# A graph neural network in fp32 on one core: two pairs of node chunks of the graph product in seven block products, results' additions and the norm's statistics re-ordered

## The chip, the core and the metric

The kernel runs on one core of one Trainium2 chip. Its engines are TensorE (PE in the profile, with its weight loads as PEld), VectorE (DVE), ScalarE (ACT), GpSimd (POOL) and SyncE (SP), which issues most of the DMAs. The metric is the device time of one execution in microseconds (us); lower is better.

## The reference, cut to what matters

Two layers work on x of 16 batches x 1024 nodes x 256 channels. The change touches layer 0: its graph product g, its queries q and keys k, and the norm that begins layer 1.

```python
h = jnp.maximum(_layernorm(x, axis=-1), 0.0)
x = x + _L0_gnn_ref(h, para, adj, kv_w)        # layer 0, below
h = jnp.maximum(_layernorm(x, axis=-1), 0.0)   # layer 1's norm
x = x + _L1_gnn_ref(h, adj, W1, ...)           # A_hat product, linear, batchnorm, relu, linear, batchnorm

# layer 0, for B=16, N=1024, C=256, 4 heads of 64
fea = jnp.transpose(h, (0, 2, 1))
c_adj = jnp.mean(fea, axis=1)
diff = c_adj[:, None, :] - c_adj[:, :, None]
A = jnp.abs(jnp.abs(jax.nn.sigmoid(diff) - 0.5) - 0.5) * 2.0
Wg = adj[None, :, :] * (A + jnp.transpose(A, (0, 2, 1))) * 0.5
g = jax.nn.relu(jnp.einsum('bcn,bnm->bcm', fea, Wg) * para.reshape(1, C, N))
q = heads(transpose(g));  k, v = heads(h @ kv_w)
attn = jax.nn.softmax(jnp.einsum('bhnd,bhmd->bhnm', q, k) * scale, axis=-1)
out = jnp.einsum('bhnm,bhmd->bhnd', attn, v)   # added to x
```

## The kernel before

All data are fp32. Each batch is worked on with its 1024 nodes in eight chunks of 128 partitions and its 256 channels in two halves. The loop over batches b has three large stages on TensorE: the attention of batch b, then `graph(b + 1)`, which makes the next batch's queries, values and keys, then linear 1 of batch b (`linear1` and `linear1_seven`), which is layer 1's A_hat product and its first linear layer.

Every engine works in the order in which the Python code issues to it: the batch loop stands in a manual schedule over all five engines, so an instruction waits for the one in front of it on its engine, and each DMA issued by SP for the one issued before it. Tiles come from pools; a tag with n buffers is used in turn, and a new tile waits until the last reader of the old one in its buffer is done.

The graph product takes, for each chunk c, a weight tile w of 128 x 1024. ScalarE makes it with Abs and Tanh, VectorE multiplies it with the chunk of adj (`weights`, L342 to L351). The tag "w4" holds five such tiles. `graph` (L375) loops over the eight chunks; before each chunk's products it runs steps handed over in the dictionary `between` (L1140 to L1152), among them the making of later w tiles, the end of the attention before it (`left`: add of the first results, collect, invert, spread, scale, add of the second results) and the norm of batch b (`norm.stats`, `norm.invert`, `norm.relu`). Each chunk has four matmuls of 128 x 128 by 128 x 512 into two PSUM tiles gps, accumulated over the eight chunks (L399).

`turn_h` transposes h: VectorE in blocks of 32, then 32 DMAs of 32 KB from the GpSimd queue into the two tiles hT, which keys and values read. The results of the attention are turned in a like way by 16 DMAs from SP (`scale`, L596 to L616) into a tile att, and added to x (L618).

After the eight chunks `queries` multiplies gps with para (two tiles from "w4", loaded by SP at chunk 5) and applies a ReLU (L416, L417). `values` makes v in two halves of 16 matmuls of 256 columns, each copied by ScalarE. From batch 2 on the keys come from seven block products instead of eight (L455 to L493), with differences of hT made by VectorE (L460 to L465) and sums of the weights loaded from DRAM: four of the products are accumulated on one running sum x in PSUM, which ScalarE copies each time a block of the result is complete in it.

[...]the tag "s" has three tiles of two banks (gps, halves of values, key products, attention scores, linear 1), "o" and "t" one bank each.

In linear 1 the A_hat product is also one of seven block products (L694 to L763). Between its products stand steps for batch b + 2: the statistics of its first norm (`prepare_start`), on x loaded by `arrive`, and the ReLU of that norm (`prepare_end`, eight ScalarE activations, L279). `arrive` reuses the tile that `leave` has stored to DRAM. ScalarE's copies L745, L749, L756 and L762 take the running sum away between the products.

Of the kernel before, what the change touches and what calls it, by code (L numbers as in the profile page):

```python
# [10 lines left out]
F32 = mybir.dt.float32  # L11
AF = mybir.ActivationFunctionType
# [5 lines left out]
P = 128  # L18
# [11 lines left out]
def fast_path(  # L30
# [143 lines left out]
    with ExitStack() as stage:  # L174
# [167 lines left out]
        def weights(b, c):  # L342


            w = w4.tile([P, N], F32, tag="w4", name=f"f_w_{b}_{c}")
            nc.scalar.activation(  # L346
                w, rows[b], AF.Abs, bias=cols[b][:, c : c + 1], scale=0.5 / C
            )
            nc.scalar.activation(w, w, AF.Tanh)  # L349
            nc.vector.scalar_tensor_tensor(w, w, 1.0, adj_t[c], ALU.subtract, ALU.mult)  # L350
            ws[b, c] = w  # L351

        hTs = {}

# [20 lines left out]
        def graph(b, between):  # L375


            gps = [ps_s.tile([P, N], F32, tag="s", name=f"f_gps_{b}_{d}") for d in range(CC)]
            hT = None
            para_t = []  # L380
            for c in range(NC):
                for step in between.get(c, ()):
                    step()
                if c == 5:
                    for d in range(CC):
                        t = w4.tile([P, N], F32, tag="w4", name=f"f_para_{b}_{d}")
                        nc.sync.dma_start(t, para_v[:, d, :])
                        para_t.append(t)
                if c == 6 and b > 1:
                    t23 = pp.tile([P, 2, 512], F32, tag="acc", name=f"f_kt23_{b}", bufs=2)  # L390
                    rest = pp.tile([P, 2, 512], F32, tag="acc", name=f"f_kt4_{b}", bufs=2)
                    sums = rest[:, 1].rearrange("p (n q) -> p n q", n=4)
                    nc.sync.dma_start(sums, kvs_d)
                w = ws.pop((b, c))
                blocks = [(d, g) for d in range(CC) for g in range(NH)]
                if b == 0 and c == 0:
                    blocks.sort(key=lambda n: n[1])
                for d, g in blocks:
                    nc.tensor.matmul(  # L399
                        gps[d][:, ts(g, 512)],  # L400
                        hs[b][:, c, ts(d, P)],
                        w[:, ts(g, 512)],
                        start=(c == 0),
                        stop=(c == NC - 1),
                    )
                if c == 0:
                    hT = hTs.pop(b)
            for step in between.get(NC, ()):
                step()
            kT = big.tile([P, CC, N], F32, tag="kT", name=f"f_kT_{b}")  # L410
            qT = big.tile([P, CC, N], F32, tag="qT", name=f"f_qT_{b}")
            v = big.tile([P, NC, C], F32, tag="v", name=f"f_v_{b}")

            def queries(d):

                nc.vector.tensor_mul(qT[:, d, :], gps[d], para_t[d])  # L416
                nc.scalar.activation(qT[:, d, :], qT[:, d, :], AF.Relu, scale=-SCALE)  # L417

            def values():
                for c4 in range(0, NC, 4):  # L420
                    ps = ps_s.tile([P, 4, C], F32, tag="s", name=f"f_vps_{b}_{c4}")
                    for i in range(4):
                        for e in range(CC):
                            nc.tensor.matmul(  # L424
                                ps[:, i, :],
                                hT[e][:, ts(c4 + i, P)],
                                kvw_t[:, e, C : 2 * C],
                                start=(e == 0),
                                stop=(e == CC - 1),
                            )  # L430
                    nc.scalar.copy(v[:, c4 : c4 + 4, :], ps)

            late = between.get("late", ())
            if b < 2:
                for step in late:
                    step()
                for d in range(CC):
                    ps = ps_s.tile([P, N], F32, tag="s", name=f"f_kps_{b}_{d}")
                    for g in range(NH):
                        for e in range(CC):  # L440
                            nc.tensor.matmul(  # L441
                                ps[:, ts(g, 512)],
                                kvw_t[:, e, ts(d, P)],
                                hT[e][:, ts(g, 512)],
                                start=(e == 0),
                                stop=(e == CC - 1),
                            )
                    nc.scalar.copy(kT[:, d, :], ps)
                    queries(d)
                values()  # L450
                return qT, kT, v

            t2, t3, t4 = t23[:, 0], t23[:, 1], rest[:, 0]  # L455
            part = lambda k, j: hT[k][:, ts(j, 512)]
            a = lambda i, k: kvw_t[:, k, ts(i, P)]
            for d in range(CC):
                queries(d)
            nc.vector.tensor_sub(t3, part(1, 1), part(0, 1))  # L460
            nc.vector.tensor_add(t2, t3, part(0, 0))
            nc.vector.tensor_sub(t4, part(1, 0), t2)
            values()
            t1 = part(0, 1)
            nc.vector.tensor_sub(t1, t1, part(0, 0))  # L465

            def mult(ps, left, right, more=False):
                nc.tensor.matmul(  # L468
                    ps, left, right, start=not more, stop=True, skip_group_check=more
                )  # L470

            c = lambda i, j: kT[:, i, ts(j, 512)]
            x = ps_s.tile([P, 512], F32, tag="s", name=f"f_kpsx_{b}")
            m7 = ps_s.tile([P, 512], F32, tag="s", name=f"f_kps7_{b}")
            m2 = ps_t.tile([P, 512], F32, tag="t", name=f"f_kps2_{b}")
            m4 = ps_o.tile([P, 512], F32, tag="o", name=f"f_kps4_{b}")
            mult(x, a(0, 0), part(0, 0))
            nc.scalar.copy(c(0, 0), x)
            mult(m2, a(0, 1), part(1, 0))
            nc.vector.tensor_add(c(0, 0), c(0, 0), m2)  # L480
            late[0]()
            mult(x, sums[:, 1], t2, True)
            nc.scalar.copy(c(1, 0), x)
            late[1]()
            mult(m7, sums[:, 2], t3)
            nc.vector.tensor_add(c(1, 0), c(1, 0), m7)
            mult(x, sums[:, 0], t1, True)
            nc.scalar.copy(c(1, 1), x)
            mult(m4, a(1, 1), t4)
            nc.vector.tensor_add(c(1, 1), c(1, 1), m7)  # L490
            nc.vector.tensor_add(c(1, 0), c(1, 0), m4)
            mult(x, sums[:, 3], part(1, 1), True)
            nc.scalar.copy(c(0, 1), x)  # L493
            return qT, kT, v

        def attention(b, qT, kT, v, hooks):

# [68 lines left out]
            def finish(g):  # L566
# [29 lines left out]
                def scale():  # L596
                    oT = oT_of.pop(g)
                    blocks = oT.rearrange("p h j c i -> p (h j c) i")
                    nc.vector.tensor_mul(
                        blocks,  # L600
                        blocks,
                        kept["recs"]
                        .rearrange("p h j c -> p (h j c)")
                        .unsqueeze(2)
                        .to_broadcast([P, 16 * HEADS // 2, 32]),
                    )
                    t = ow.tile(
                        [P, HEADS // 2, 4, 4, 32], F32, tag="att", name=f"f_att_{b}_{g}"
                    )
                    for a in range(4):  # L610
                        for j in range(4):
                            nc.sync.dma_start(
                                t[ts(j, 32), :, a].rearrange("r h c i -> r h (c i)"),
                                oT[ts(a, 32), :, j].rearrange("r h c i -> r h (c i)"),
                            )
                    kept["att"] = t  # L616
# [430 lines left out]
        with tc.manual_schedule(engines={ENG.PE, ENG.Activation, ENG.DVE, ENG.Pool, ENG.SP}):  # L1047
# [73 lines left out]
            for b in range(B):  # L1121
# [35 lines left out]
                if b + 1 < B:  # L1157
                    if 0 < b < B - 2:
                        thirds = load_thirds(b)
                    qkv = graph(b + 1, between)  # L1160
                    if b == 0:
                        for step in scale[4:]:
                            step()
                        thirds = make_thirds(b)
                if b + 2 < B:
# [1 line left out]
                        b,  # L1167
                        norm.h,
                        thirds,
                        lambda: prepare_start(b + 2),  # L1170
                        lambda: prepare_end(b + 2),
                        lambda: (prepare_row(b + 2), again(b + 1)),
                    )
# [932 lines left out]
```

## Time and profile before

| what | value |
|---|---|
| time, median of 3 runs | 2425.27 us (2425.07 to 2425.58) |
| the profiled execution | 2425.91 us |
| its span, first to last instruction | 2424.1 us |
| granted TensorE clock, mean | 0.995 |
| PE / DVE / ACT / POOL busy in the span | 2384.8 / 1781.2 / 1325.8 / 308.6 us |
| graph matmuls (L399), records | 1024, busy 444.7 us |
| one batch of the loop, graph(3) to graph(4) | 389.1 to 522.4 us of the span |
| of it VectorE busy in the attention, 466.0 to 522.4 | 53.3 us |

The page lists busy time per engine, then the chain of work that ended last, followed back from the last instruction. One program matmul in fp32 appears as two records. A line number such as L399 is that of the kernel printed above. Times inside the trace count from the span's start; a window row gives start:end, its length, and then for each engine the busy time with the number of instructions in brackets, the TensorE clock, the share of the DMA engines and GB/s.

### The profile page before, as it was taken

To read this page: it belongs to the slowest core of one execution; us is meant where nothing else is said; L and a number is where in the kernel's file an instruction comes from. 1 tells how busy PE (TensorE), PEld (TensorE's weight loads), DVE (VectorE), ACT (ScalarE), POOL (GpSimd) and SP (SyncE) were. 2 spreads that over 40 slices of the span, in tenths; PEclk is the share of its full clock that TensorE was granted. 3 is DMA by queue.
4 is the path that set the end of the run, shared out by engine and by line. 5 is a ranking of instruction groups with operands and counts; after the bars stand their busy time and mean duration, and the time that the engine had idled before them with its cause. 6 is when DMAs were issued, how large, how long until landed. Compare 5 with 4: busy or idle time off the path is not lost.

```text
span 2424.1 us, 24651 instructions
## 1 busy us (share of the span) xinstructions
PE 2384.8 (98%) x8034; PEld 1050.7 (43%) x8034; DVE 1781.2 (73%) x2442; ACT 1325.8 (55%) x1932; POOL 308.6 (13%) x547
## 2 busy tenths in 40 slices
PE   8999999999999999999999999999999999999995
PEld 4453444434343434444343434344443434444444
DVE  6878778685959586786859595877868596757766
ACT  6845555464646455554646464555546465446654
POOL 2030202021020302020200203020202011000000
PEclk9999999999999999999999999999999999999998
DMA  5041414222332414142323324142423222355569
GB/s 187 9 140 61 152 61 126 87 88 74 115 95 62 146 61 152 61 126 87 89 73 115 95 63 146 61 152 61 126 87 88 73 68 85 101 192 195 176 239 375
DMA packets 176633, 275.76 MB, mean 114 GB/s; under 512 B 37872, under 2 KB 121328, under 8 KB 176496
## 3 DMA queue, kind: packets, MB, share of 16 engines
q1 hardware_dynamic: 156336, 241.55, 30.7%
q0 software_dynamic: 15552, 15.77, 2.5%
q10 hardware_dynamic: 4608, 16.78, 1.7%
q8 instruction: 66, 1.08, 0.2%
q14 instruction: 71, 0.58, 0.1%
HBM read 169.35 MB, written 71.10 MB: 99 GB/s over the span
## 4 chain that ended last, share of the span: by engine, by line
PE 93%; DVE 3%; DMA 2%; issue 1%; SPq 1%; POOL 0%; ACT 0%; DVEq 0%; ACTq 0%; POOLq 0%
PE f_s L507 17%; PE f_o L548 17%; PE f_gps L399 17%; PE f_aps L704 16%; PE f_zps L810 6%; PE f_vps L424 4%; PE f_zx L1326 4%; PE f_zm L1326 3%; PE f_kpsx L468 2%; PE f_kps L468 1%; DVE f_acc L524 1%; PE f_outps L1546 1%; PE f_z2ps L1264 1%; PE f_kps L441 1%; PE f_zps L892 1%
## 5 line engine op out<-in xcount | busy, mean ns | idle before, releaser
L515 ACT ACTIVATE f_p<-f_s 128x1024 f32<-128x1024 f32 x512 | 477.3, 1046 | 151.8 <-PE f_s L507 151.7
L524 DVE TENSOR_TENSOR f_acc<-f_acc,f_p 128x1024 f32<-128x1024 f32 x384 | 470.5, 1225 | 41.1 <-ACT f_p L515 0.5
L507 PE MATMUL f_s<-f_qT,f_kT 64*128 64x512 f32 x2048 | 456.8, 596 | 0.0
L548 PE MATMUL f_o<-f_p,f_v 128*64 128x512 f32 x2048 | 453.6, 595 | 0.0
L399 PE MATMUL f_gps<-f_w,f_h_a 128*128 128x512 f32 x1024 | 444.7, 594 | 0.3 <-DVE f_w L337 0.3
L369 POOL DMA_DIRECT2D f_hT<-f_hQ x480 | 235.9, 499 | 1221.7 <-PE f_gps L399 1170.8
L507 PEld LDWEIGHTS f_s<-f_qT,f_kT 64*128 64x128 f32 x2048 | 190.7, 185 | 263.6 <-ACT f_p L515 117.1
L399 PEld LDWEIGHTS f_gps<-f_w,f_h_a 128*128 128x128 f32 x1024 | 192.8, 190 | 247.0 <-issue 230.0
L548 PEld LDWEIGHTS f_o<-f_p,f_v 128*64 128x64 f32 x2048 | 141.4, 137 | 304.3 <-issue 254.2
L350 DVE SCALAR_TENSOR_TENSOR f_w<-f_w,f_adj 128x1024 f32<-128x1024 f32 x127 | 153.8, 1212 | 39.1 <-ACT f_w L349 39.1
L346 ACT ACTIVATE f_w<-f_row,f_col 128x1024 f32<-128x1024 f32 x127 | 147.0, 1157 | 29.3 <-DMA f_row<-frow 28.5
L279 ACT ACTIVATE f_h_b<-f_x,f_shift_b,f_rstd_b 128x256 f32<-128x256 f32 x128 | 67.9, 594 | 162.5 <-DVE f_shift_b L264 162.5
L349 ACT ACTIVATE f_w<-f_w 128x1024 f32<-128x1024 f32 x127 | 134.3, 1057 | 4.0
L704 PE MATMUL f_aps<-f_ahatT,f_hs 128*128 128x512 f32 x256 | 115.1, 592 | 0.0
L424 PE MATMUL f_vps<-f_kvw,f_hT 128*128 128x256 f32 x512 | 113.4, 379 | 0.2 <-DVE f_qT L416 0.2
L704 PE MATMUL f_aps<-f_ahatT,f_h_b 128*128 128x512 f32 x256 | 112.7, 593 | 0.0
L704 PE MATMUL f_aps<-f_t,f_hs 128*128 128x512 f32 x256 | 112.5, 592 | 0.0
L279 ACT ACTIVATE f_h_a<-f_x,f_shift_a,f_rstd_a 128x256 f32<-128x256 f32 x126 | 73.8, 587 | 62.6 <-DVE f_shift_a L264 62.6
L424 PEld LDWEIGHTS f_vps<-f_kvw,f_hT 128*128 128x128 f32 x512 | 97.2, 190 | 20.6 <-issue 7.4
L521 DVE TENSOR_TENSOR f_acc<-f_p,f_p 128x1024 f32<-128x1024 f32 x64 | 76.2, 1191 | 15.3 <-ACT f_p L515 15.3
L590 ACT COPY f_recs<-f_rec 32x32 f32<-32x32 f32 x128 | 31.5, 246 | 98.7 <-DVE f_rec L582 97.5
L575 ACT COPY f_parts<-f_red 32x64 f32<-32x64 f32 x128 | 39.0, 305 | 78.5 <-DVE f_red L540 77.3
(230 smaller groups left out, 2705.7 us busy)
## 6 DMA issues: line engine op xcount, KB each, us to landing
f_t<-ft SPq DMA_DIRECT2D x84, 512.0 KB, 6.9
fz<-f_z SPq DMA_DIRECT2D x64, 512.0 KB, 9.9
f_x<-in_x_dram SPq DMA_DIRECT2D x31, 1024.0 KB, 5.9
f_zb<-fz SPq DMA_DIRECT2D x42, 512.0 KB, 4.2
f_para<-in_L_gnn_para_dram SPq DMA_DIRECT2D x32, 512.0 KB, 4.5
f_att<-f_oT SPq DMA_DIRECT2D x512, 32.0 KB, 1.9
fx<-f_x SPq DMA_DIRECT2D x16, 1024.0 KB, 6.5
f_hT<-f_hQ POOLq DMA_DIRECT2D x480, 32.0 KB, 2.6
```

The costliest lines, as they stand in the source:

```text
L346: nc.scalar.activation(w, rows[b], AF.Abs, bias=cols[b][:, c : c + 1], scale=0.5 / C)
L350: nc.vector.scalar_tensor_tensor(w, w, 1.0, adj_t[c], ALU.subtract, ALU.mult)
L369: queue.dma_start(to[ts(k, 32), ts(a, 32 * NC)], t[ts(a, 32), k].rearrange("i c r -> i (c r)"),)
L399: nc.tensor.matmul(gps[d][:, ts(g, 512)], hs[b][:, c, ts(d, P)], w[:, ts(g, 512)], start=(c == 0), stop=(c == NC - 1),)
L424: nc.tensor.matmul(ps[:, i, :], hT[e][:, ts(c4 + i, P)], kvw_t[:, e, C : 2 * C], start=(e == 0), stop=(e == CC - 1),)
L507: nc.tensor.matmul(ps[:, e, :], kT[rows_e, pair, ts(m, P)], qT[rows_e, pair, ts(g, 512)], start=True, stop=True,)
L515: nc.scalar.activation(p, ps, AF.Exp)
L524: nc.vector.tensor_add(acc_of[s], acc_of[s], p)
L548: nc.tensor.matmul(o_of[s][e * HD : (e + 1) * HD, :], v[:, m, ts(2 * pair + e, HD)], p[:, e, :], start=(m == 0), stop=(m == NC - 1),)
L704: nc.tensor.matmul(ps, left[:, m, :], right(m), start=not more and m == 0, stop=(m == KH - 1), skip_group_check=more,)
L810: nc.tensor.matmul(ps[i], left[:, ts(i, P)], right, start=not more, stop=True, skip_group_check=more,)
L1326: nc.tensor.matmul(ps, left[:, m, :], right[:, m, :], start=start and m == 0, stop=(m == 1), skip_group_check=not start,)
```

## The change

For batches 2 to 15 `graph` is replaced by `graph_seven`; batches 0 and 1 keep `graph`. The statements' order in it is the order on each engine.

- Chunks 0 to 3 are accumulated as before. Chunks 4 to 7 form two pairs n = 0, 1. For each pair the 2 x 2 block product (channel halves by node halves, summed over the two chunks) is made from seven products with sums s of h and differences t of w, and the products of the two pairs are accumulated.
- s1 to s4 (256 columns each) are made by VectorE in the tag "sums". Of the t's, t2 and t3 lie in the still unused kT, t1 and t4 overwrite parts of w.
- A running sum in the "t" bank is copied by ScalarE three times into the still unused v (`room`), and m7 stands in the "o" bank. VectorE then adds m7 twice, adds gps, and multiplies by para, which is loaded in one DMA into qT itself, ahead of the results' DMAs.
- The ReLU of the queries is done later: one half among the key products, the other in linear 1 (`todo`), for the last batch both among the key products.
- The first results' addition comes after the t's, the second in front of the multiplication of the second half by para, behind the keys' differences. The second results' tile takes the tag "oT" in place of "att".
- The norm's statistics, root, shifts and ReLU go by halves: chunks 0 to 3 after the graph product, chunks 4 to 7 among the key products, its ReLU at their end. `leave` and `arrive` are issued among the key products.

```diff
+        def graph_seven(b, left, norm, last):
+            gps = [ps_s.tile([P, N], F32, tag="s", name=f"f_gps_{b}_{d}") for d in range(CC)]
+            add0, collect, invert, spread, scale, add1 = left
+            h = hs[b]
...
+            turn_h(b)
+            differences(b, 2)
+            masked(b, 2)
+            collect()
+            invert()
+            differences(b, 3)
+            masked(b, 3)
+            differences(b, 4)
+            qT = big.tile([P, CC, N], F32, tag="qT", name=f"f_qT_{b}")
+            nc.sync.dma_start(qT, para_v)
+            spread()
+            scale()
+            masked(b, 4)
+            plain(0)
+            differences(b, 5)
+            masked(b, 5)
...
+            room = v.rearrange("p (n k) c -> p n (k c)", n=4)
+            nc.vector.tensor_sub(s3, a(0, 0), a(1, 0))
+            nc.vector.tensor_add(s1, a(1, 0), a(1, 1))
+            nc.vector.tensor_sub(s2, s1, a(0, 0))
+            nc.vector.tensor_sub(s4, a(0, 1), s2)
+            plain(1)
+            differences(b, 6)
+            masked(b, 6)
+            make_t3(0)
+            make_t1(0)
+            plain(2)
+            differences(b, 7)
+            masked(b, 7)
+            make_t2(0)
+            plain(3)
...
+            make_t3(1)
+            make_t1(1)
+            make_t2(1)
...
+            m1(0)
+            m2(0)
+            m1(1)
+            nc.scalar.copy(room[:, 0], x)
+            m_7(0)
+            m3(0)
+            m2(1)
+            make_t4(0)
+            make_t4(1)
+            m6(0)
+            m_7(1)
+            m3(1)
+            m6(1)
+            nc.scalar.copy(room[:, 2], x)
+            m4(0)
+            m4(1)
+            m5(0)
+            m5(1)
+            nc.scalar.copy(room[:, 1], x)
+            add0()
+            nc.vector.tensor_add(room[:, 2], room[:, 2], m7)
+            norm.stats(0, 4)
+            norm.invert(0, 4)
+            nc.vector.tensor_add(room[:, 3], room[:, 1], m7)
+            for d in range(CC):
+                nc.vector.tensor_add(both(d), both(d), gps[d])
...
+            nc.vector.tensor_mul(qT[:, 0, :], both(0), qT[:, 0, :])
+            norm.shifts(0, 4)
+            norm.relu(0, 4, False)
+            copy0, copy1 = values(b, hT, v)
+            copy0()
+            nc.vector.tensor_sub(kt3, part(1, 1), part(0, 1))
+            nc.vector.tensor_add(kt2, kt3, part(0, 0))
+            nc.vector.tensor_sub(kt4, part(1, 0), kt2)
+            nc.vector.tensor_sub(kt1, kt1, part(0, 0))
+            add1()
+            nc.vector.tensor_mul(qT[:, 1, :], both(1), qT[:, 1, :])
+            norm.stats(4, NC)
+            norm.invert(4, NC)
...
             nc.vector.tensor_add(c(0, 0), c(0, 0), k2)
-            late[0]()
+            leave(b - 1)
+            arrive(b + 1)
             mult(x, sums[:, 1], kt2, True)
             nc.scalar.copy(c(1, 0), x)
-            late[1]()
+            todo.pop(0)()
             mult(m7, sums[:, 2], kt3)
             nc.vector.tensor_add(c(1, 0), c(1, 0), m7)
             mult(x, sums[:, 0], kt1, True)
             nc.scalar.copy(c(1, 1), x)
+            copy1()
             mult(k4, aw(1, 1), kt4)
             nc.vector.tensor_add(c(1, 1), c(1, 1), m7)
+            norm.shifts(4, NC)
             nc.vector.tensor_add(c(1, 0), c(1, 0), k4)
             mult(x, sums[:, 3], part(1, 1), True)
             nc.scalar.copy(c(0, 1), x)
-            return qT, kT, v
+            if last:
+                todo.pop(0)()
+            norm.relu(4, NC, False)
+            return (qT, kT, v), todo
...
-                        [P, HEADS // 2, 4, 4, 32], F32, tag="att", name=f"f_att_{b}_{g}"
+                        tag="att" if g == 0 else "oT",
...
-                    qkv = graph(b + 1, between)
+                    if b == 0:
+                        qkv = graph(b + 1, between)
+                        todo = []
+                    else:
+                        qkv, todo = graph_seven(b + 1, left, norm, b + 2 == B)
...
-                        lambda: prepare_start(b + 2),
+                        lambda: ([step() for step in todo], prepare_start(b + 2)),
```

The products and differences that `graph_seven` calls, for pair n, where a(i, k) is channel half i of h in the pair's chunk k, and part_w(n, k, j) node half j of that chunk's w:

```python
make_t3: t3[n] = part_w(n, 1, 1) - part_w(n, 0, 1)
make_t1: t1[n] = part_w(n, 0, 1) - part_w(n, 0, 0)   # in place
make_t2: t2[n] = part_w(n, 1, 1) - t1[n]
make_t4: t4[n] = part_w(n, 1, 0) - t2[n]             # in place
m1: x += a(0,0) part_w(n,0,0)      m2: gps[0] half 0 += a(0,1) part_w(n,1,0)
m_7: m7 += s3 t3[n]                m3: gps[0] half 1 += s4 part_w(n,1,1)
m6: x += s2 t2[n]                  m4: gps[1] half 0 += a(1,1) t4[n]
m5: x += s1 t1[n]
```

## The prediction

> **What bounds the kernel now.** I read the page's busy shares first, then the chain of waits that ended last, then the waits of TensorE, and then one batch by stages and engine by engine.
>
> ```profile
> PE 2384.8 (98%) x8034; PEld 1050.7 (43%) x8034; DVE 1781.2 (73%) x2442; ACT 1325.8 (55%) x1932; POOL 308.6 (13%) x547
> PE 93%; DVE 3%; DMA 2%; issue 1%; SPq 1%; POOL 0%; ACT 0%; DVEq 0%; ACTq 0%; POOLq 0%
> PE f_s L507 17%; PE f_o L548 17%; PE f_gps L399 17%; PE f_aps L704 16%; PE f_zps L810 6%; PE f_vps L424 4%; PE f_zx L1326 4%; PE f_zm L1326 3%; PE f_kpsx L468 2%; PE f_kps L468 1%; DVE f_acc L524 1%; PE f_outps L1546 1%; PE f_z2ps L1264 1%; PE f_kps L441 1%; PE f_zps L892 1%
> ```
>
> [...] Here the chain says it too: 93% of it is PE. From graph(2) on the chain repeats every 133.3 us, one batch; this is graph(3) with what follows (start, length, what):
>
> ```profile
> 389.15 27.66 PE f_gps L399 x64
> 416.82 6.91 PE f_vps L424 x32
> ...
> 430.04 24.03 PE f_aps L704 x56
> 454.08 10.30 PE f_zps L810 x24
> ```
>
> The reader is to see that these pieces abut. The windows of that batch (graph product, values, keys, two linear-1 parts, attention; columns PE, PEld, DVE, ACT, POOL busy) have PE busy in every microsecond:
>
> ```profile
> 389.10:416.70 27.60, 27.60 (x67) 12.29 (x66) 20.25 (x37) 13.49 (x20) 17.38 (x33) 1.00 0.76 235
> 416.70:423.60 6.90, 6.90 (x34) 6.07 (x33) 3.88 (x6) 4.38 (x6) 0.00 (x0) 1.00 0.28 99
> 423.60:429.90 6.30, 6.30 (x16) 2.40 (x15) 2.81 (x5) 4.65 (x8) 0.00 (x0) 1.00 0.11 16
> 429.90:453.90 24.00, 24.00 (x57) 10.62 (x56) 8.94 (x27) 7.00 (x20) 1.64 (x1) 1.00 0.17 61
> ```
>
> So matmuls taken out shorten the run one for one, as long as VectorE (DVE) keeps up: it is busy 20.25+3.88+2.81 = 26.9 of the 40.8 us from graph product to last key product.
>
> **Prices.** [...] 32 graph matmuls in the program are 64 records in 27.66 us, 0.864 us each. [...] an fp32 add: 0.69 us at 512 (trace 0.69), 1.22 at 1024 (trace 1.22)[...]. Independent neighbours start closer together in the trace (0.60 and 1.13 us).
>
> **The change, part by part,** for each of the 14 batches 2 to 15 (graph(0) and graph(1) keep the old form).
>
> 1. TensorE. Four chunks stay at 4 matmuls each; two pairs take 7 products of 2 matmuls. 16+14 = 30 instead of 32: 2 x 0.864 = 1.73 us less, 24.2 us in all. Certain if PE never waits.
>
> 2. VectorE adds, per batch: four sums of 256 (1.7), eight differences of 512 (5.5), two additions of 512 (1.4), two of 1024 out of PSUM (2.4): 11.0 us. With 26.9 that is 37.9 of a stage of 39.1. It fits with 1.2 us to spare, so order decides; I lay it out from 389.15, with durations of the rows above. Transposes to 393.3, mask 2 to 394.5, reciprocals to 395.7, mask 3 to 396.9, scale to 398.3 (it waits for four ScalarE copies, 1.0), mask 4 to 399.4, mask 5 to 400.6, four sums to 402.25, mask 6 to 403.4, t3, t1 to 404.75, mask 7 to 405.9, t2 and the second pair's t3, t1, t2 to 408.6, t4 twice to 409.9. ScalarE's Abs and Tanh of chunks 5, 6, 7 end at 399.3, 401.4, 403.6; they wait for the buffers of w0, w1, w2, which PE gives back at 392.6, 396.1, 399.5: no delay. PE needs: mask 4 at 403.0, mask 5 at 403.9, mask 6 at 404.7, t3 at 405.6, mask 7 at 407.3, t2 at 408.2, second t3 at 409.0, second t2 at 410.8, t4 at 411.6. The least margin is 1.3 us. So no wait; the graph product ends at 389.15 + 30 x 0.864 = 415.1.
>
> 3. ScalarE copies the shared sum out of PSUM three times (0.59 each). Two lie under three and two matmuls (2.6, 1.7 us); the third follows the last product.
>
> 4. What follows the graph product is a chain with no work of PE to hide it but values (6.9) and two key products. Copy 415.3-415.9, addition of m7 to 416.65, two additions from PSUM to 417.9 and 419.0 (the first frees the bank of the second half of values, needed at 418.5: margin 0.6), times para to 420.15, shifts 420.06, four ReLU of the norm (416.10 to 418.18 before: 2.08) to 422.3, copy of values to 423.3, copy of the first key product to 423.75. PE wants that at 415.1 + 6.9 + 1.72 = 423.7. A wait of about 0.15 a batch: 2.1 us in all. This is the term without cover: each microsecond later here is one lost. I take bounds of 0 (copies overlap more) and 0.7 (eight VectorE and ScalarE steps each 0.09 longer).
>
> 5. Keys: the second copy of values now stands behind the third key copy and ends at 428.3; the first linear-1 product reuses its bank and may start at 428.3-428.4, when the keys end anyway. Nothing, at most 0.1.
>
> 6. Norm in halves. First half's statistics fall where VectorE idles (411 to 416). The second half comes after keys' differences, results' addition and para: shifts at 428.9, four ReLU to 431.2, where before they ended at 428.05. Its chunk 4 is needed 3.43 after linear 1 starts, 431.8: ready 429.7. Behind the ReLU, SP's queue holds the load of the next x; it issued at 428.08 and landed 5.5 us later, now 431.2 + 5.5 = 436.7. Statistics and the root take 3.28 + 2.02: 442.0. They must be there when VectorE has added m7 in linear 1, 443.0, so 1.0 of margin; behind that lie eight ReLU on ScalarE and the copy before the last product, whose margin is 450.48 - 449.92 = 0.56. Nothing, with 1.5 us in reserve.
>
> 7. Queues. One load of para (1 MB) goes ahead of the 16 DMAs of the results on SP, in the loads' rush (DMA share 0.98 to 1.04 from 392 to 400), instead of two behind them; the results then wait for it and end near 413, three or four microseconds later, but their addition (before: 410.9, waiting 2.8 for them) now stands at 423. The store of x moves from 412.15 to 424.1, needs about 5 to 7 us and ends before 431.2. POOL's 32 transposing DMAs may end 1 to 2 us later than 411.6; the first values need only the first quarter, keys' differences the rest at 420.2. [...] these DMAs took 496 to 558 ns with two-input VectorE work beside them. Nothing, at most 1 a batch.
>
> 8. Last batch (15). No linear 1 stands between keys and attention: one query ReLU (1.04) and four norm ReLU (2.08) come ahead of the first exponential, which was ready 1.15 after the scores start. It starts some 2.5 later; three score buffers hide part. Once, about 2.3 us; bounds 0 and 3.
>
> Sum: 24.2 - 2.1 - 2.3 = 19.8 us. The profiled execution took 2425.91 (span 2424.1 and 1.8 around it), 0.64 above the median of the runs: 2406.1 there, 2405.5 as median.
>
> **Rivals.**
>
> A. The chain of step 4 is longer than I sum. For: no slack, VectorE nearly full, all of it cross-engine hand-overs. Against: every duration and hand-over is taken from this trace. At 1 us a batch in place of 0.15: 12 us less gain, 2417.
>
> B, slower. VectorE becomes the bound. The place: the second half's shifts come late, the next x loads late behind the ReLU, ScalarE's copy before linear 1's last product (L756) is late, and PE stops there. The price: each microsecond past the 1.5 of reserve costs one a batch. It is slower than before by 0.2% once it loses (19.8 + 4.9)/14 = 1.76 us a batch, that is with the norm 3.3 late, a fifth of the 16 us between the graph product's end and that ReLU. At 3.7 late, 1.0 of it paid in step 4 already and 1.2 at L756, 2.2 x 14 = 31: 2436. For: 37.9 of 39.1 us, and VectorE in order. Against: VectorE's idle stretches before 416 (1.5 and 1.1 us in my layout) take up early delays.
>
> C. Everything hides, the last batch too: 24.2, 2401.1.
>
> That the change doesn't do what it says: the built order shows 30 graph matmuls in each of these batches, so I give it nothing.
>
> **How the numbers follow.** Forecast 0.68 (its own range 2402 to 2410: waits of 0 to 0.4 a batch), A 0.18, C 0.05, B 0.09. The range 2401 to 2414 holds the forecast, C and A's milder half. 0.2% (4.9 us) is what a measurement of this kernel can tell from no change. Faster: forecast, C and nearly all of A, 0.88; same 0.04, from A's far end and B's beginning; slower 0.08, from B.
>
> **What would show it.** Period of a batch 131.6 to 131.8 instead of 133.3 us; graph stage 25.9 without a wait on VectorE; a short wait at the second shared key product for ScalarE; x loads issued 3 us later against the graph's start; no PE wait at the last aps product. A PE wait there, or before the second half of values, or on the t's, proves me wrong.

## The result, and the profile after

The change takes 2405.0 us, the median of 4 runs (2404.46 to 2406.27), against 2425.43 us for the kernel before in the same comparison (4 runs, 2425.07 to 2427.64): a ratio of 0.9915, 95% interval 0.9897 to 0.9932. The profiled execution took 2404.77 us, its span 2403.0.

The page's row of busy times and, from the chain that ended last, its shares by engine:

```profile
PE 2363.1 (98%) x7978; PEld 1040.6 (43%) x7978; DVE 1920.7 (80%) x2694; ACT 1346.3 (56%) x1974; POOL 313.8 (13%) x561
PE 96%; DMA 2%; ACT 1%; DVE 1%; issue 0%; SPq 0%; POOL 0%; DVEq 0%; ACTq 0%; POOLq 0%
```

TensorE lost 56 records and 21.7 us of busy time, VectorE gained 139.5 us (10.0 in each of the 14 batches), and the chain still runs over TensorE. The work that VectorE took over costs it over six times what TensorE saved, and that is free only as long as no matmul comes to wait for it: 0.69 us more cost nothing at one place (e3a) and 0.72 at another (e3b).

The chain of waits of one batch, graph(3) and what follows it (start, length, what). The trace after runs 1.59 us ahead of the one before at this place, so 1.59 is added to a time of after before it is compared with one of before.

```profile
387.56 13.93 PE f_gps L474 x32
...
413.51 6.91 PE f_vps L447 x32
420.41 0.86 PE f_kpsx L636 x2
...
422.13 1.05 PE f_kpsx L636 x2
...
426.78 24.09 PE f_aps L888 x56
...
519.23 10.93 PE f_gps L474 x25
```

The graph product lasts 413.51 - 387.56 = 25.95 us, where it had 416.82 - 389.15 = 27.67. The keys last 426.78 - 420.41 = 6.37 instead of 430.04 - 423.73 = 6.31: the third piece, the second product on the running sum, takes 1.05. It was not free before either, as the chain of the kernel before and its ScalarE timeline show (the copy there is the one this product needs):

```profile
425.44 1.00 PE f_kpsx L468 x2
```

```profile
424.67 0.59 ACT L478 COPY f_kT<-f_kpsx 128x512 f32<-128x512 f32 x1
```

So 0.05 of the 1.05 is new. The first part of linear 1 has 24.09 instead of 24.03. From one graph product to the next it is 519.23 - 387.56 = 131.67 us instead of 133.28: 1.61 a batch, 0.11 less than the 1.72 by which the graph product became shorter.

The windows of graph product, values and keys (busy time and count of PE, PEld, DVE, ACT, POOL; clock, DMA share, GB/s):

```profile
387.50:413.40 25.90, 25.90 (x63) 11.57 (x62) 24.06 (x39) 13.96 (x20) 15.77 (x33) 1.00 0.78 233
413.40:420.30 6.90, 6.90 (x34) 6.09 (x33) 5.97 (x8) 2.34 (x5) 1.00 (x1) 1.00 0.04 13
420.30:426.70 6.40, 6.40 (x16) 2.31 (x15) 6.37 (x16) 4.74 (x7) 1.01 (x1) 1.00 0.49 166
```

PE is busy throughout, and from the graph product to the keys VectorE is busy 24.06 + 5.97 + 6.37 = 36.4 of 39.2 us. In the keys it has practically no gap left.

Thirteen such periods, graph(2) to graph(15), account for 21.0 us. The last batch lost 0.54: from graph(15) to linear 1 it took 97.77 us (1967.94 to 2065.71) where it had 97.23 (1988.93 to 2086.16), although it too has two matmuls less. TensorE's timeline (start, length, operation, in brackets the idle time before it and what ended it) shows the place:

```profile
2007.10 2.85 PE L687 MATMUL f_s<-f_qT,f_kT 64*128 64x512 f32 x12
2011.66 4.78 PE L687 MATMUL f_s<-f_qT,f_kT 64*128 64x512 f32 x20 [1.72 <-ACT f_p L695]
```

The last attention's scores stop after 12 records because no score buffer is free. ScalarE's timeline says why:

```profile
2007.69 1.06 ACT L648 ACTIVATE f_qT<-f_qT 128x1024 f32<-128x1024 f32 x1
2008.64 2.06 ACT L279 ACTIVATE f_h_b<-f_x,f_shift_b,f_rstd_b 128x256 f32<-128x256 f32 x4
2010.61 7.39 ACT L695 ACTIVATE f_p<-f_s 128x1024 f32<-128x1024 f32 x8
```

Five ReLU stand ahead of the first exponential: one of the queries (L648) and four of the norm (L279). In total the loop and the last batch gain 20.45 us up to 2065.71 (2086.16 before); the span became shorter by 21.1, and the other 0.65 lies in the stages behind.

### The profile page after: what moved, and what is told of

Same layout as the page of the kernel before. It is cut to its first block, busy times and chain, and to the rows that moved or that the text cites. A ratio compares the mean times of both kernels' runs of the same rounds, so it can differ in the third digit from the quotient of the medians.

```text
span 2403.0 us, 24814 instructions
## 1 busy us (share of the span) xinstructions
PE 2363.1 (98%) x7978; PEld 1040.6 (43%) x7978; DVE 1920.7 (80%) x2694; ACT 1346.3 (56%) x1974; POOL 313.8 (13%) x561
## 3 DMA queue, kind: packets, MB, share of 16 engines
q8 instruction: 65, 1.06, 0.2%
## 4 chain that ended last, share of the span: by engine, by line
PE 96%; DMA 2%; ACT 1%; DVE 1%; issue 0%; SPq 0%; POOL 0%; DVEq 0%; ACTq 0%; POOLq 0%
PE f_s L687 19%; PE f_o L728 19%; PE f_aps L888 16%; PE f_gps L474 8%; PE f_zps L994 6%; PE f_vps L447 4%; PE f_gps L556 4%; PE f_zx L1514 4%; PE f_gpsx L556 3%; PE f_zm L1514 3%; PE f_kpsx L636 2%; PE f_gps L401 2%; PE f_kps L636 1%; DMA f_z<-fx 1%; PE f_outps L1734 1%; PE f_zps L1076 1%
## 5 line engine op out<-in xcount | busy, mean ns | idle before, releaser
L474 PE MATMUL f_gps<-f_w,f_h_a 128*128 128x512 f32 x448 | 196.0, 596 | 0.0
L350 ACT ACTIVATE f_w<-f_row,f_col 128x1024 f32<-128x1024 f32 x127 | 147.1, 1158 | 14.1 <-DMA f_row<-frow 13.3
L474 PEld LDWEIGHTS f_gps<-f_w,f_h_a 128*128 128x128 f32 x448 | 84.1, 190 | 111.7 <-issue 99.0
L279 ACT ACTIVATE f_h_b<-f_x,f_shift_b,f_rstd_b 128x256 f32<-128x256 f32 x128 | 66.3, 590 | 77.0 <-DVE f_shift_b L264 77.0
L279 ACT ACTIVATE f_h_a<-f_x,f_shift_a,f_rstd_a 128x256 f32<-128x256 f32 x126 | 73.8, 587 | 50.8 <-DVE f_shift_a L264 50.8
L1017 ACT ACTIVATE f_z<-f_zps,f_b 128x512 f32<-128x512 f32 x60 | 37.9, 683 | 75.3 <-PE f_zps L994 75.3
## 6 DMA issues: line engine op xcount, KB each, us to landing
f_qT<-in_L_gnn_para_dram SPq DMA_DIRECT2D x14, 1024.0 KB, 13.3
```

The costliest lines, as they stand in the source:

```text
L350: nc.scalar.activation(w, rows[b], AF.Abs, bias=cols[b][:, c : c + 1], scale=0.5 / C)
L474: nc.tensor.matmul(gps[d][:, ts(g, 512)], h[:, c, ts(d, P)], w[:, ts(g, 512)], start=(c == 0), stop=(c == PLAIN - 1),)
```

## The experiments

The theory: each batch gains two matmuls' time, and the loss comes from two places that can be pointed at: one copy order at the keys (some 0.1 a batch), the last batch's ReLU (some 2 us once), and nothing else, since VectorE's work up to the graph product's end and the norm's lateness both have reserve. Rivals: the gain comes from the order of the stages and not from the products; VectorE is the bound already; the norm's second half is as good as late.

**e1: the last batch's ReLU behind the first exponential.** The remaining query ReLU and the norm's four are put into the list that runs after the attention's first step of scores and exponentials; the last load of x, which stood behind them, moves with them.

```diff
             if last:
-                todo.pop(0)()
-            norm.relu(4, NC, False)
+                todo.append(lambda: norm.relu(4, NC, False))
+            else:
+                norm.relu(4, NC, False)
...
+                    hooks[0] = [*todo, lambda: again(b)]
...
-                    again(b + 1)
```

> The last batch alone: its second query ReLU and the norm's second four ReLU stand behind the first step of scores and exponentials instead of ahead of them, and the load of x moves behind them. My theory: the last attention lost 2.2 us to them (58.5 us from its first score to the next product, 56.3 before), so about 2402.8 as median, and no PE wait of 1.7 us in that attention. Rival (the last attention is held up by something else, say the wider range of VectorE work before it): unchanged, 2405.

Measured: 2402.25 us (2401.86 to 2402.58), ratio 0.9903 (0.9887 to 0.9920). ScalarE's timeline there:

```profile
2008.06 7.44 ACT L696 ACTIVATE f_p<-f_s 128x1024 f32<-128x1024 f32 x8 [0.48 <-PE f_s L688]
2015.31 1.12 ACT L648 ACTIVATE f_qT<-f_qT 128x1024 f32<-128x1024 f32 x1
2016.25 2.12 ACT L279 ACTIVATE f_h_b<-f_x,f_shift_b,f_rstd_b 128x256 f32<-128x256 f32 x4
```

In the chain, the scores start at 2006.95 in e1 and at 2007.18 in after. The exponential starts 2008.06 - 2006.95 = 1.1 us after them instead of 2010.61 - 2007.18 = 3.4, and TensorE no longer waits there. From first score to linear 1 it is now 2006.95 to 2063.29, 56.34 us, what the kernel before had; after had 2065.71 - 2007.18 = 58.5. The lines of the kernel before, then that of after:

```profile
2029.82 7.07 PE f_s L507 x32
...
2086.16 24.23 PE f_aps L704 x56
```

```profile
2065.71 24.23 PE f_aps L888 x56
```

The 2.2 us are those five ReLU.

**e2: the new order with all eight chunks in the old form.** Additions, norm, queries' ReLU and queues stay as in the change; sums, differences and seven products go, gps is multiplied by para directly.

```diff
-            plain(3)
+            for c in range(3, NC):
+                plain(c)
...
-            nc.scalar.copy(room[:, 0], x)
...
-            nc.vector.tensor_add(both(d), both(d), gps[d])
...
-            nc.vector.tensor_mul(qT[:, 0, :], both(0), qT[:, 0, :])
+            nc.vector.tensor_mul(qT[:, 0, :], gps[0], qT[:, 0, :])
```

> The new order and the norm in halves, but all eight chunks plain: 32 graph matmuls, no sums, differences or room additions, VectorE's 11 us a batch gone. My theory (only the two matmuls count): period 133.3 us a batch, the last attention's 2.2 us still lost, 2427 to 2428. Rival (part of the gain comes from the new order and the halves): below 2420, with a period clearly under 133.2.

Measured: 2429.57 us (2428.48 to 2430.15), ratio 1.0015 (1.0008 to 1.0022). Its chain:

```profile
389.41 27.66 PE f_gps L474 x64
...
426.64 1.09 PE f_kps L539 x2
...
430.39 24.09 PE f_aps L791 x56
...
522.84 7.49 PE f_gps L474 x17
```

The period is 522.84 - 389.41 = 133.43 us, 0.15 more than before. So the order alone brings no gain; 0.15 x 14 and the last batch's 2.2 make 4.3 us of loss, within the measured interval (1.9 to 5.3). The gain is that of the seven products, 133.43 - 131.67 = 1.76 a batch between these two kernels, which share the order.

The loss was somewhat above what was expected, and the 0.15 isn't that of the change. The first part of linear 1 has the 24.09 of after, so that 0.06 belongs to the order. But the fourth key piece takes 1.09 instead of 0.86, which after doesn't show, and the third has 0.94 instead of the 1.05 of after. VectorE's timeline of e2 (L531 is the second multiplication by para) ends just before that product starts, and the trace gives it as what the product's weight load waited for:

```profile
425.33 1.22 DVE L531 TENSOR_TENSOR f_qT<-f_gps,f_qT 128x1024 f32<-128x1024 f32 x1
```

In e2 this multiplication still reads gps out of PSUM, and the product's bank is the second gps; in after the additions L612 have read both by 417.30. So e2 answers whether the order makes the gain (no), and not what the order costs to a tenth of a microsecond.

**e3: VectorE 0.7 us more, early or in the chain.** One difference is made twice ahead of the products (e3a), or one addition of m7 is made twice behind them (e3b); both repeat work and leave the result as it is.

```diff
             make_t2(1)
+            make_t2(1)
```

```diff
             nc.vector.tensor_add(room[:, 3], room[:, 1], m7)
+            nc.vector.tensor_add(room[:, 3], room[:, 1], m7)
```

> One more VectorE difference of 512 (0.69 us, the second pair's t2 made twice) ahead of the last t's, before the graph product ends. My theory: VectorE's two idle stretches before the first addition out of the shared sum take it up; period 131.67, time 2405. Rival (VectorE is the bound of the stage, 36.4 of 39.2 us busy): 0.6 to 0.7 us more a batch, about 2414.

> The same length of work (one addition of 512, room 3 made twice, 0.69 us) behind the graph product's end, in the chain from the last copy to the first key copy. My theory: no cover, 0.65 to 0.72 us more a batch, all as a PE wait at the second shared key product or the second half of values; period 132.3 to 132.4, 2414 to 2415. Rival (VectorE has slack there too): unchanged, 2405.

Measured: e3a 2404.44 us (2404.07 to 2404.81), ratio 0.9916 (0.9887 to 0.9945), period 131.67, as in after. e3b 2414.48 us (2413.37 to 2414.66), ratio 0.9953 (0.9934 to 0.9973), period 520.86 - 388.47 = 132.39. First VectorE's timeline of after, then that of e3a:

```profile
408.39 1.22 DVE L804 TENSOR_TENSOR f_x<-f_x,f_att 128x1024 f32<-128x1024 f32 x1
410.73 0.69 DVE L606 TENSOR_TENSOR f_v<-f_v,f_gps 128x512 f32<-128x512 f32 x1 [1.12 <-ACT f_v L599]
414.16 0.69 DVE L609 TENSOR_TENSOR f_v<-f_v,f_gps 128x512 f32<-128x512 f32 x1 [0.94 <-ACT f_v L604]
414.95 2.35 DVE L612 TENSOR_TENSOR f_v<-f_v,f_gps 128x1024 f32<-128x1024 f32 x2
```

```profile
405.82 1.42 DVE L529 TENSOR_TENSOR f_kT<-f_w,f_w 128x512 f32<-128x512 f32 x2
410.36 0.69 DVE L607 TENSOR_TENSOR f_v<-f_v,f_gps 128x512 f32<-128x512 f32 x1 [0.78 <-ACT f_v L600]
```

In after VectorE stands idle twice, 1.12 and 0.94 us, each time for a copy of ScalarE that a matmul releases. In e3a the added difference shortens the first of these, here to 0.78 because VectorE had come to this graph product 0.38 us earlier; in graph(8) it is 0.76 instead of 1.49. The addition behind it comes 23.17 us after the graph product's start in both kernels (410.73 - 387.56, 410.36 - 387.19). Behind the second idle time VectorE has none until the shifts on which ScalarE's ReLU, copy of values and first key copy follow. For that key copy TensorE waits; e3b's list of waits and timeline:

```profile
PE f_kpsx L637 <- ACT f_kT L653: 5.4, 14, 0.4
```

```profile
414.25 7.33 PE L447 MATMUL f_vps<-f_kvw,f_hT 128*128 128x256 f32 x32
423.69 1.12 PE L637 MATMUL f_kpsx<-f_kt,f_kt 128*128 128x512 f32 x2 [0.39 <-ACT f_kT L653]
```

The wait stands once in each of the 14 batches; the values take 7.33 instead of 7.07, because the bank of their second half, which VectorE's first addition L613 of e3b reads, comes free later too: that addition ends 3.55 us after the values start (417.80 - 414.25), where half of them takes 3.45 (6.91 / 2), and in after L612's first ended 2.83 after (416.17 - 413.34). So 0.26 of the 0.72 is lost there and the rest at the key product. An addition of 0.69 us costs 0.72 a batch here and nothing some 8 us earlier.

**e4: the norm's second half later.** The statistics of chunks 4 to 6 are made twice (e4a), or those of chunks 4 to 7 three times (e4b), both on VectorE among the keys; the result stays as it is.

```diff
+            norm.stats(4, 7)
             norm.stats(4, NC)
```

```diff
             norm.stats(4, NC)
+            norm.stats(4, NC)
+            norm.stats(4, NC)
```

> Statistics of three chunks made twice before the second half of the norm: its ReLU about 1.2 us later. My theory: 1.6 us of reserve behind it (1.1 before the next norm's shifts, 0.55 before linear 1's last product), so nothing: period 131.67, 2405. Rival (the reserve is smaller, or the chunks are needed at once by the second product): up to 1.2 us a batch, 2422.

> Statistics of the second half made three times: its ReLU 3.4 us later. My theory: the reserve of 1.6 us is spent and the rest is lost in every batch that has a linear 1 behind it, 1.8 us each of 13, period 133.4, 2428 to 2430, and the wait is at linear 1's last product for ScalarE's copy (or earlier at its second product). Rival (the late norm matters only through VectorE's own time): about 2405 to 2410.

Measured: e4a 2404.57 us (2404.12 to 2405.02), ratio 0.9916 (0.9887 to 0.9945), period 131.67. e4b 2427.66 us (2425.77 to 2429.25), ratio 1.0009 (1.0002 to 1.0017), period 133.26 in the mean of the 13 (133.04 to 133.55). ScalarE in e4a:

```profile
428.15 2.07 ACT L279 ACTIVATE f_h_b<-f_x,f_shift_b,f_rstd_b 128x256 f32<-128x256 f32 x4 [0.94 <-DVE f_shift_b L264]
```

ReLU and the load of x behind it come 1.04 later against the graph product (40.78 instead of 39.74 us after it starts), and the next norm's shifts still come at 53.7, as in after: the load wasn't what they waited for. In e4b ReLU is 3.49 later (432.35 - 389.12 = 43.23), and the chain that ended last turns off TensorE here, over the load, and comes back at the last product of linear 1's first part:

```profile
432.35 1.57 ACT f_h_b L279 x3
433.94 5.87 DMA f_x<-in_x_dram
...
445.31 4.78 ACT f_h_a L279 x16
450.09 0.48 ACT f_u L942
...
450.61 3.70 PE f_aps L890 x8
```

TensorE's list has both stops:

```profile
PE f_aps L890 <- ACT f_h_b L279: 8.6, 13, 0.7
PE f_aps L890 <- ACT f_u L942: 5.2, 13, 0.7
```

The first is the second product of linear 1's first part, which reads the late chunk itself, the second its last product; the first is the longer stop in the mean (8.6 / 13 = 0.66 against 5.2 / 13 = 0.40 us). Of 3.49 us of lateness 1.59 are paid a batch, so 1.9 a batch were reserve. This is the mechanism of the prediction's slower rival: the rival named the last product, and step 6 gave a margin for chunk 4 as well. It needs the norm over 3 us later than the change puts it.

**e5: the copies of values one place later.** ScalarE's first copy of values goes behind the first key copy, the second to the second key copy; the query ReLU that stood there goes to linear 1 (in the last batch to where the second copy was).

```diff
-            copy0()
...
             nc.scalar.copy(c(0, 0), x)
+            copy0()
...
             nc.scalar.copy(c(1, 0), x)
-            todo.pop(0)()
+            copy1()
...
             nc.scalar.copy(c(1, 1), x)
-            copy1()
+            if last:
+                todo.pop(0)()
```

> ScalarE's order among the keys changed: first key copy ahead of the first copy of values, the second copy of values ahead of the third key copy, the query ReLU both later. My theory: each batch still loses 0.05 to 0.12 us to ScalarE there and at the first linear-1 product (period 131.67 where 133.28 less 1.73 is 131.55); 0.7 to 1.7 us less, 2403.3 to 2404.3, period 131.55 to 131.62. Rival (these are fixed hand-over costs of the shared sum): period unchanged at 131.67, or longer since m7 now waits for the copy of values.

Measured: 2403.0 us (2402.5 to 2403.74), ratio 0.9906 (0.9890 to 0.9923), period 131.51 in the mean of the 13 (519.59 - 388.09 = 131.50 here). ScalarE's timeline of after, then that of e5, then e5's chain:

```profile
420.53 0.99 ACT L455 COPY f_v<-f_vps 128x1024 f32<-128x1024 f32 x1
421.42 0.58 ACT L652 COPY f_kT<-f_kpsx 128x512 f32<-128x512 f32 x1
```

```profile
421.84 0.59 ACT L651 COPY f_kT<-f_kpsx 128x512 f32<-128x512 f32 x1 [0.68 <-PE f_kpsx L635]
```

```profile
422.66 0.94 PE f_kpsx L635 x2
423.60 0.92 PE f_kps L635 x2
424.52 0.88 PE f_kpsx L635 x2
...
427.20 24.03 PE f_aps L889 x56
```

In after the first key copy starts right behind the copy of values and ends at 422.0, 1.59 us after the keys start; in e5 the copy of values no longer stands ahead and the key copy ends 1.49 after (422.43 - 420.94). The third key piece takes 0.94 instead of 1.05, and linear 1 has its 24.03 again. The rival was right in part: the fourth piece now waits for the copy of values and takes 0.92 instead of 0.86, but the fifth takes 0.88 instead of 0.94. Together that is 0.16 a batch, somewhat more than expected. The period is 1.77 below that of before: the change's whole gain and, since the third piece had 1.00 before, a little more.

What these pieces cost is not a fixed price of going on with a running sum. Compared over the traces, a pair of records that had to wait ends 1.17 or 1.18 us after the end of the operation it waited for: 423.18 after 422.00 in after, 426.44 after 425.26 in before, 423.60 after 422.43 in e5 (all the first key copy), 424.52 after 423.34 in e5 (the copy of values), 427.73 after 426.55 in e2 (VectorE's multiplication). The pair itself lasts 0.86, so from this difference, 1.17 - 0.86, I estimate that an operation is hidden when it ends some 0.31 us ahead of the product that needs it, and that each 0.1 us later costs 0.1; in e2 a copy that ended 0.46 ahead (427.27 to 427.73) cost nothing. In e5 the first key copy starts 0.04 after the product it copies, takes 0.59 and ends 0.23 ahead of the pair that needs it, with a single product of 0.86 between the two: 0.94 - 0.86 = 0.08 us remain.

**e6: e1 and e5 together.**

> Both edits, of the last batch's ReLU and of ScalarE's order among the keys. My theory: the two gains add, 2401 to 2402. Rival: at least one of them does nothing, 2403 or more.

Measured: 2400.73 us (2400.47 to 2400.91), ratio 0.9898 (0.9881 to 0.9914), just below what was expected. e1 and e5 had 2.75 and 2.0 us less than the change; together it is 4.27 less (differences of medians, which are no surer than some tenths of a microsecond), so the two gains add as nearly as these runs can tell. This version is faster than both kernels.

## Why the prediction was right

The forecast of 2405.5 us (2406.1 for the profiled execution) met 2405.0 (2404.77), in the main by the way it described; two of its small terms were off in opposite directions (4 and 5), and that they made up for each other in part is luck.

1. *TensorE, 1.73 a batch.* Measured 27.67 - 25.95 = 1.72 in the graph product, without a wait. Each of the program's matmuls stands in the traces as two records, 0.86 us together.

2. *VectorE, 11.0 us more, least margin 1.3.* The forecast put 37.9 us of VectorE into the stage; the windows have 36.4. By the busy row VectorE gained 10.0 us a batch, not 11.0: adding single durations overstates, since independent neighbours start closer together than they last (two key additions of after, L661 and L666, start 0.60 us apart and last 0.68). A further 0.69 is the last key addition, which now stands behind the stage. The least margin, at the weight tile of chunk 6, was 1.06 (ready at 402.15, used at 403.21). The 1.7 us for four sums of 256 columns was the author's estimate. A straight line through the additions in the trace before, 0.69 us at 512 columns and 1.22 at 1024, gives an estimate of about 0.42 for each, and the trace after agrees:

```profile
399.33 0.42 DVE L506 TENSOR_TENSOR f_gs<-f_h_a 128x256 f32<-128x256 f32 x1
```

The two idle stretches, forecast as 1.5 and 1.1, are 1.12 and 0.94 in this batch (1.49 and 0.95 in graph(8)). e3a shows that another difference early on costs nothing.

3. *ScalarE's three copies.* No matmul of the graph product waits for them; its products on the running sum take 0.86 each like all others.

4. *The chain without cover, 0.15 a batch.* The first key copy was forecast to end at 423.75, and ended at 422.0 + 1.59 = 423.6. The stop is at the product named, and against a free product it costs 1.05 - 0.86 = 0.19. But the kernel before already paid 1.00 - 0.86 = 0.14 there, which the forecast didn't count: the price of the change is 0.05, a third of the 0.15. That the chain has no slack is shown by e3b, which lost 0.72 of 0.69 us.

5. *Second copy of values, nothing, at most 0.1.* Measured 0.06, in linear 1's first piece (24.09). By the trace the weight load of that product waits for this copy in each of the 13 batches with a linear 1 behind the keys. The copy ends 0.26 us ahead of the product (426.52 to 426.78), which by the 0.31 estimated in e5 is 0.05 too late. Steps 4 and 5 together stand at 0.11 over what keys and linear 1 had before (6.31 and 24.03), where 0.15 was forecast, and e5 removes both.

6. *Norm in halves, nothing, 1.5 us in reserve.* VectorE's timeline of after has the two shifts:

```profile
426.94 0.16 DVE L264 SCALAR_TENSOR_TENSOR f_shift_b<-f_mv_b,f_rstd_b 128x4 f32<-128x4 f32 x1
441.28 0.16 DVE L264 SCALAR_TENSOR_TENSOR f_shift_a<-f_mv_a,f_rstd_a 128x8 f32<-128x8 f32 x1
```

With 1.59 added they are at 428.5 and 442.9; forecast were 428.9 and 443.0. The load of x is issued 41.84 us after the graph product starts instead of 38.93, 2.9 later, where 3 was forecast. The reserve is above 1.0 (e4a) and about 1.9 (e4b), a little more than forecast.

7. *Queues, nothing.* The last of the results' DMAs is issued at 410.83 + 1.59 = 412.4 (forecast near 413). GpSimd's last transposing DMA is issued 25.4 us after the graph product starts instead of 22.9: 2.4 later, where 1 to 2 were forecast, and 5.5 us before the keys' differences read what it brings. With VectorE busy 24.06 of 25.9 us instead of 20.25 of 27.6, each of these 32 DMAs took GpSimd 496 to 558 ns, as before.

8. *Last batch, 2.3 once.* Measured 2.2; e1 gives it back.

The sum was 24.2 - 2.1 - 2.3 = 19.8. The traces have 14 x 1.72 = 24.1, less 0.11 in each of the 13 full periods (1.4), less 2.2: 20.5 (20.45 measured up to the end of the last attention), and 0.65 in the stages behind it. Those 0.65 are within the scatter: from the end of the last attention to the end of the span the ten traces, whose code is the same there, have 337.2 to 338.3 us, with 337.9 in before and 337.3 in after.

Of the rivals, A (a longer chain) needed about 1 us a batch more, which at e3b's price (0.72 for 0.69) is one and a half additions more. B needed the norm over 3 us later; e4b shows its mechanism and its price, and stands with 3.49 just past the point where the gain is gone. C (everything hides) isn't what this kernel does, but e6 comes to it: 2400.73 against 2401.1.

## What to carry to other kernels

Where one engine's busy pieces abut over a whole period, as here, count its instructions taken out at full price (here 1.72 us of the 1.73 counted), and then look for the few places where the engines that took the work over have no idle time left before the next product: an instruction of 0.69 us cost nothing ahead of such an idle stretch and 0.72 us behind it. Look at the end of a loop by itself, since work moved into the next stage stands, in the last round, ahead of something else. Before a wait is charged to a change, see whether the same product already waited before it: the forecast charged 0.15 where only 0.05 was new. When everything just fits, the order of the copies on a helper engine counts: here it was worth 2.0 us, as much as the forecast put down for the waits of all batches (2.1).

## What the runs showed of the hardware

- The root on GpSimd over 128 x 4 took 1.01 to 1.03 us in the loop of after, over 128 x 8 1.64 to 1.66 in that of before (2.63 at its first use there): half the width took 0.61 to 0.63 of the time.
- A matmul pair of 0.86 us that had to wait ended 1.17 or 1.18 us after the end of what it waited for, a ScalarE copy (after, before, e5) or a VectorE multiplication (e2). From this, less the 0.86, the hand-over is an estimated 0.31 us. A pair one product behind the copy of its own running sum took 0.94 us or more, except where the product between had waited itself (0.88 behind 0.92 in e5, 0.86 behind 1.09 in e2).
- The 1 MB load of para, issued in the loads' rush ahead of the results' DMAs, took 13.3 us to land in the median (5.3 to 14.5), and x's loads of the same size 6.8.
- ScalarE and SP kept the order of issue where the runs moved something. With five ReLU issued ahead of it the first exponential of the last attention started 3.4 us after the scores (after), with them behind it 1.1 us (e1). As the load of x moved, the load issued by SP behind it came 0.48 us after it each time (429.40 and 429.88 in after, 430.25 and 430.73 in e4a, 433.94 and 434.42 in e4b).
